# A diffusion transformer of four layers: the rotary step on three engines, modulations with their operands exchanged, and an MLP that may begin beside attention

## The chip, the cores and the metric

The kernel runs on one core of one Trainium2 chip. A core has five engines with instruction queues of their own: TensorE (PE, matrix products, with weight loads in a row of their own, PEld), VectorE (DVE), ScalarE (ACT, activation functions from tables), GpSimd (POOL) and SyncE (SP, which here only issues DMAs). Each takes its queue in order and waits on semaphores for the others. TensorE writes to PSUM, eight banks of 128 x 512 floats. The metric is the device time of one execution in microseconds, the median of three.

## The reference, cut to what matters

Sixteen samples of 256 tokens and width 256 pass through four layers in sequence. All have 16 heads of 16 columns and are computed in fp32; a context of 77 tokens per sample feeds the cross attentions.

```python
# layer 0: modulated norm, masked self attention with rotary position, cross attention, MLP
x_norm = _ln(x, norm1_w) * (1 + sc_msa) + sh_msa
q, k = _apply_rope(q, cos, sin), _apply_rope(k, cos, sin)
x = x + g_msa * self_out;  x = x + g_x * cross;  x = x + g_mlp * mlp_out
# layer 1: modulated cross attention          layer 2: self attention, cross attention, MLP, modulated
# layer 3: the rotary layer again, with rotary queries and keys in the cross attention too
q = _rope((xn @ q_w.T).reshape(B, L, N_HEADS, HEAD_DIM))
k = _rope((context @ k_w.T).reshape(B, L_ctx, N_HEADS, HEAD_DIM))
h = jax.nn.gelu(xn @ ffn_w1.T + ffn_b1, approximate=False)
x = res + (h @ ffn_w2.T + ffn_b2)
```

A modulation is a product of the 16 condition vectors with a 256 x 512 weight: a shift and a scale for every sample and column. A rotary step is `t * cos + swap(t) * sin`, where `swap` exchanges the two halves of each head's 16 columns (the sign lies in the sine table).

## The kernel before, in words

The work has six stages. Stage a is layer 0's attentions, b its MLP, c the attentions of layers 1 and 2, d layer 2's MLP, e layer 3's attentions, f its MLP. In a and e all 16 self attentions come first and the 16 cross attentions after them; priorities grow in that order.

The order of instructions is made by a planner (`Order`, line 71). Every step is a task with an engine, an estimated duration, dependencies, and holds on numbered buffers: `b` is the eight PSUM banks, `kq` five buffers for an attention's keys and queries or for MLP and modulation weights, `qk` four for rotated projections, `rope` two, `ec` two for exponentials or for an MLP's hidden rows, `xn`, `y` and `xr` one each. `solve` (line 101) lets the engines run in estimated time; a TensorE step is chosen by priority, others by when they became ready. The result is written out as one fixed program, so other durations or dependencies shuffle the whole program. The planner's durations know nothing of activation tables.

The steps that the change and the prediction speak of:

- **Norm of a sample** (`norm_tasks`, 476): statistics on VectorE (L460, L461), the reciprocal root (L466, L467) and scaling (L491) on GpSimd, a transpose of blocks on VectorE (L519), two DMAs through DRAM (L524, L528), and the modulation on ScalarE (L539).
- **Modulation** (`modulation`, 368): for each of four groups of 128 columns the weight is TensorE's stationary side and the 16 conditions stream (L382); VectorE adds the bias (L387, L389, L392). There are ten, `0a` to `3m`.
- **Rotary** (`rotate_tasks`, 663): projections into a bank (L619, or L684 for the 77 context tokens), then `turns` on VectorE: the product with the cosines (L696) and two with the sines (L699), all reading the bank; then `plus` on GpSimd (L704). `turn_back` (711) transposes the sum (L724), and ScalarE takes it to `kq` (L635, L651).
- **Attention** (`attention`, 731): scores for the row maxima (L844, L856; reductions L870, L874, L878), the maxima through DRAM into the operands (L888 to L895), scores again (L937), the exponential on ScalarE (L949, L951), value products (L960), division (L969 to L986), output product (L619), addition to `x_sb` (L1016, or L1026 to L1031).
- **MLP** (`mlp`, 1037): the norm waits for the norms of all attentions of the stage before (`bar0`). The first product (L1059), gelu on ScalarE (L1064) and second product (L1010) start at `open_h`, which waits for `barrier`, the join of all exponentials of the stage before. In turn the exponentials of the next stage wait for all gelus. Exponential, tanh gelu and exact gelu need three different function tables, and the load of a table is an instruction in ScalarE's queue.

The program prints the functions with the profile's line numbers:

Of the kernel before, what the change touches and what calls it, by code (L numbers as in the profile page):

```python
# [13 lines left out]
ALU = mybir.AluOpType  # L14
AX = mybir.AxisListType

B, N, D, H, HD, LC, FF = 16, 256, 256, 16, 16, 77, 1024
P = 128
# [42 lines left out]
class Task:  # L61
    __slots__ = ("eng", "dur", "run", "deps", "take", "prio", "rp", "left", "ready", "outs", "held", "start", "end", "no", "since", "kind", "more",
                 "lat", "first", "mb")
# [10 lines left out]
class Order:  # L74
# [4 lines left out]
    PATIENCE = 2.0  # L79
    FAVOUR = 3.0  # L80
    PER_MB = 2.7
    def __init__(self, caps):
# [17 lines left out]

    def solve(self):
        import heapq
        caps = self.caps
        loose = {k: list(range(n)) for k, n in caps.items()}
        free, waiting, events, result = {}, {}, [], []
# [34 lines left out]
        def choose(cand):  # L140

            lone = None
            for t in cand:
                if t.rp is None:
                    return [t]
                mates = [u for u in cand if u.rp == 1 - t.rp and room(t, u.take)]
                if mates:
                    return [t, min(mates, key=lambda u: (u.kind == t.kind, u.prio, u.no))]
                if lone is None:
                    lone = t  # L150
                    if t.since is None:
                        t.since = now
            if lone is not None and (now >= lone.since + self.PATIENCE - 1e-9 or not events):
                return [lone]
            return None

        while n_done < len(self.tasks):
            progress = True
            while progress:
                progress = False  # L160
                for eng in list(waiting):
                    if eng != "NO" and free.get(eng, 0.0) > now + 1e-9:
                        continue
                    cand = [t for t in waiting[eng] if t.ready <= now + 1e-9]
                    cand.sort(key=lambda t: (t.prio, t.no) if eng == "PE" else (not t.first, t.prio, t.no) if eng in ("SP", "NO") else
                              (not t.first, t.ready - self.FAVOUR * any(h.tag == "b" for h in t.held), t.prio, t.no))
# [28 lines left out]
def pixart_kernel(ctx: ExitStack, tc: tile.TileContext, x, cond_t, ctx_in, mask_c, mask_s, tables, vecs, rows,  # L195
# [172 lines left out]
    def modulation(name, src, col, shift_at, scale_at, c_t, bias, norm=None, gate=None, deps=(), prio=0, gprio=None):  # L368
        hw, hm, s = Hold("kq"), Hold("b"), {}
        m = mods[name] = const.tile([P, 4, B], F32, name=f"mod_{name}")  # L370
# [5 lines left out]
        def mults():  # L376
            ps = psum(hm)
            s["ps"] = ps[:, 0:4 * B].rearrange("p (s b) -> p s b", b=B)
            for i, at in enumerate((shift_at, scale_at)):
                for c in range(NC):  # L380
                    for k in range(NC):
                        nc.tensor.matmul(s["ps"][:, 2 * i + c, :], lhsT=s["w"][:, k, at + c * P:at + (c + 1) * P],  # L382
                                         rhs=c_t[:, k, :], start=(k == 0), stop=(k == NC - 1))

# [277 lines left out]
    def rotate_tasks(s, key, ws, xT, src_t, n, half, uses, name, prio):  # L662
# [6 lines left out]
        for group in ([list(range(nt))] if len(ws) == 1 else [[t] for t in range(nt)]):  # L669
# [16 lines left out]

            def turns(group=group, u=u, hr=hr):
                r1 = u["r1"]
                r2 = u["r2"] = buf(hr)
                hn = width // HD  # L690
                for i, t in enumerate(group):
                    tt = (t * P % half) // P
                    pv, v1, v2 = (a[0:r, i * width:(i + 1) * width].rearrange("q (h w) -> q h w", w=HD)
                                  for a in (u["p"], r1, r2))
                    cs = tabT[0:r, tt, 0, :].unsqueeze(1).to_broadcast([r, hn, HD])
# [341 lines left out]
    def mlp(b, name, wv, h_w, w_t, eps, mod, func, b1, pre_add, gate, prio, barrier, before):  # L1037
# [343 lines left out]
```

## Time and profile before

| | |
|---|---|
| median of 3 runs | 2617.77 us (2614.37 to 2619.29) |
| the profiled execution | 2619.31 us, span 2617.4 us |
| mean granted TensorE clock | 0.991 |
| GpSimd scaling L491 | 320 of 1469 ns |
| rotary add L704, 128x512 | 80 of 1276 ns |
| rotary products L696, 128x512; L699, 128x256 | 64 of 681 ns; 128 of 414 ns |
| modulation product L382 | 160 recorded passes, median 263 ns |
| copy of a bank by ScalarE, 128x512 (L1024) | 16 of 575 ns |
| table loads | 6 of 1283 ns |

An fp32 matmul shows as two recorded passes. A busy time counts a pass with its latency, so overlapping passes are merged in sums and not in means. Some matmul records are missing from a trace. An instruction's name is its line in the kernel, its output tile and its inputs. Times in the timeline are from the start of the span.

### The profile page before, as it was taken

How to read it: one execution, taken by the hardware profiler on the slowest of the kernel's cores; microseconds unless marked ns; L12 is line 12 of the kernel's file. 1: busy time of each engine (PE TensorE's matmuls, PEld its weight loads, DVE VectorE, ACT ScalarE, POOL GpSimd, SP SyncE). 2: the span in 40 equal slices, each digit the busy share in tenths (PEclk: the TensorE clock that was granted, in tenths of full speed). 3: DMA queues.
4: the chain of work that ended last, by engine and by line, in shares of the span. 5: the costliest groups of instructions: out<-in, count | busy, mean ns of one | idle time of the engine just before them, and what ended most of it. 6: DMA issues, size and time to landing. Idle time of an engine off the chain costs nothing. (4 is left out here: it accounts for less than half of the span.)

```text
span 2617.4 us, 71563 instructions
## 1 busy us (share of the span) xinstructions
PE 2562.5 (98%) x29192; PEld 1677.9 (64%) x29192; DVE 1596.0 (61%) x4489; ACT 1284.3 (49%) x2559; POOL 1138.9 (44%) x1429
## 2 busy tenths in 40 slices
PE   8999999999999899999999999999999999998999
PEld 4555555556888656555556567888555555566888
DVE  6788886775130567777777784111878887885100
ACT  2555555564333456565556564232455555554322
POOL 5344434566552355333335566432233334557310
PEclk9999999999999899999999999999999999999999
DMA  5110111224221121111111123111100001121110
GB/s 173 31 32 26 35 33 40 69 79 136 69 78 53 40 70 51 57 52 40 40 41 46 55 79 106 60 61 41 36 28 28 28 28 38 46 77 57 57 57 29
DMA packets 159809, 144.08 MB, mean 55 GB/s; under 512 B 24648, under 2 KB 124216, under 8 KB 158712
## 3 DMA queue, kind: packets, MB, share of 16 engines
q1 hardware_dynamic: 159480, 139.51, 17.1%
q8 instruction: 229, 3.75, 0.6%
q14 instruction: 100, 0.82, 0.1%
HBM read 91.86 MB, written 47.61 MB: 53 GB/s over the span
## 5 line engine op out<-in xcount | busy, mean ns | idle before, releaser
L951 ACT ACTIVATE ec<-bank 128x512 f32<-128x512 f32 (+1 forms) x1152 | 611.6, 596 | 505.1 <-PE bank L844 300.2
L937 PE MATMUL bank<-kq 32*128 32x256 f32 (+1 forms) x5120 | 638.3, 395 | 4.9 <-ACT ec L949 2.7
L491 POOL TENSOR_SCALAR xn<-x_sb,mv,rstd 128x256 f32<-128x256 f32 x320 | 452.6, 1469 | 112.4 <-DVE y L519 101.3
L937 PEld LDWEIGHTS bank<-kq 32*128 32x128 f32 (+1 forms) x5120 | 360.3, 167 | 186.5 <-issue 96.7
L844 PE MATMUL bank<-kq 32*128 32x512 f32 x1536 | 446.8, 634 | 1.6 <-ACT ec L951 0.8
L874 DVE TENSOR_REDUCE mx<-bank 128x2 f32<-128x512 f32 x544 | 342.3, 680 | 59.3 <-PE bank L844 58.2
L1064 ACT ACTIVATE ec<-bank,vec 128x256 f32<-128x256 f32 x384 | 159.9, 467 | 403.1 <-PE bank L1059 365.5
L960 PE MATMUL bank<-ec,v 128*32 128x256 f32 (+1 forms) x5120 | 351.7, 385 | 5.2 <-ACT ec L951 2.9
L1059 PE MATMUL bank<-xT,kq 128*128 128x256 f32 x1536 | 344.1, 381 | 0.0
L1010 PE MATMUL bank<-kq,ec 128*128 128x256 f32 x1536 | 340.2, 379 | 0.0
L1059 PEld LDWEIGHTS bank<-xT,kq 128*128 128x128 f32 x1536 | 291.9, 191 | 42.1 <-issue 2.8
L1010 PEld LDWEIGHTS bank<-kq,ec 128*128 128x128 f32 x1536 | 291.2, 190 | 41.3 <-issue 2.1
L982 POOL TENSOR_TENSOR od<-ts,rec 128x128 f32<-128x128 f32 x448 | 170.9, 403 | 319.5 <-DVE rec L976 319.3
L519 DVE STREAM_TRANSPOSE y<-xn 128x512 f32<-128x512 f32 x158 | 110.6, 700 | 306.9 <-DMA yd<-y 255.2
L960 PEld LDWEIGHTS bank<-ec,v 128*32 128x32 f32 (+1 forms) x5120 | 156.4, 110 | 158.6 <-issue 39.4
L878 DVE TENSOR_REDUCE mx<-bank 128x4 f32<-128x308 f32 x512 | 211.6, 468 | 41.5 <-PE bank L937 30.0
L870 DVE CUSTOM_DVE_ANT_0 junk<-bank,ctx 128x256 f32<-128x256 f32 x448 | 189.0, 422 | 51.6 <-PE bank L844 22.1
L969 DVE STREAM_TRANSPOSE ts<-bank 128x512 f32<-128x512 f32 x224 | 157.8, 705 | 68.0 <-PE bank L960 57.9
L466 POOL TENSOR_SCALAR rstd<-mv 128x2 f32<-128x2 f32 x160 | 37.9, 237 | 352.8 <-DVE mv L461 281.3
L704 POOL TENSOR_TENSOR qk<-qk,rope 128x512 f32<-128x512 f32 (+1 forms) x96 | 113.7, 1185 | 175.5 <-DVE rope L699 118.7
L856 PE MATMUL bank<-kq 32*128 32x154 f32 x2048 | 166.4, 307 | 3.3 <-ACT ec L951 1.1
L844 PEld LDWEIGHTS bank<-kq 32*128 32x128 f32 x1536 | 136.6, 183 | 40.0 <-ACT ec L951 24.6
(162 smaller groups left out, 3255.9 us busy)
## 6 DMA issues: line engine op xcount, KB each, us to landing
yd<-y SPq DMA_DIRECT2D x158, 256.0 KB
xr<-yd SPq DMA_DIRECT2D x158, 256.0 KB
kq<-in_mod_dram SPq DMA_DIRECT2D x10, 512.0 KB
cin<-in_ctx_in_dram SPq DMA_DIRECT2D x36, 128.0 KB
x_sb<-in_x_dram SPq DMA_DIRECT2D x16, 256.0 KB
gb<-gate_g0m SPq DMA_DIRECT2D x16, 256.0 KB
gb<-gate_g2a SPq DMA_DIRECT2D x16, 256.0 KB
gb<-gate_g2m SPq DMA_DIRECT2D x16, 256.0 KB
```

The costliest lines, as they stand in the source:

```text
L491: nc.gpsimd.tensor_scalar(to, of, s["mv"][:, t, 0:1], s["rstd"][:, t:t + 1], ALU.subtract, ALU.mult)
L844: ls.append(lambda ps=ps, R=R, keys=keys: nc.tensor.matmul(ps.rearrange("p (s k) -> p s k", k=N), lhsT=s["qx"][R, 0, g, t * P:(t + 1) * P] ...
L856: ls.append(lambda ps=ps, R=R, keys=keys, tt=tt: nc.tensor.matmul(ps[:, 2 * tt * n:2 * (tt + 1) * n].rearrange("p (s k) -> p s k", k=n), l ...
L870: nc.vector.tensor_tensor_reduce(junk, u[i][:, i2 * N:(i2 + 1) * N], mb[:, t, :], -1.0, 3.0e38, ALU.add, ALU.min, m[:, i2, g, t:t + 1])
L874: nc.vector.tensor_reduce(m[:, :, g, t], u[i].rearrange("p (s k) -> p s k", k=N), AX.X, ALU.max, negate=True)
L878: nc.vector.tensor_reduce(m[:, :, g].rearrange("p s t -> p t s"), u[i][:, 0:4 * n].rearrange("p (t s k) -> p t s k", s=2, k=n), AX.X, ALU. ...
L937: (lambda ps=u[i], R=R, q=q: nc.tensor.matmul(ps[0:rows_n, q * N:(q + 1) * N], lhsT=s["kz"][R, q, g, kc * P:kc * P + rows_n], rhs=s["qx"][ ...
L951: nc.scalar.activation(e, u[i][0:rows_n], AF.Exp)
L960: nc.tensor.matmul(u5["p"][32 * r:32 * r + 32, 1 - q, :], lhsT=s["v"][0:rows_n, kc, 8 * g + 2 * r + 1 - q, :], rhs=s["e", g, kc, r][0:rows ...
L982: nc.gpsimd.tensor_tensor(ov[:, :, HD * i:HD * i + HD], ts[:, i, :, HD * i:HD * i + HD], rec[:, i, :].unsqueeze(2).to_broadcast([P, N // 3 ...
L1010: nc.tensor.matmul(u["p"][:, t, :], lhsT=lhsT(k, t), rhs=w()[:, k, :], start=(k == 0), stop=(k == nk - 1))
L1059: nc.tensor.matmul(u["p"][:, j, :], lhsT=wv["w1"][:, k, f * P:(f + 1) * P], rhs=s["xT"][:, k, :], start=(k == 0), stop=(k == NC - 1))
```

## The change

Three edits, one program.

1. Rotary: the bank is copied to SBUF by ScalarE, which frees the bank; GpSimd multiplies with the sines from the copy; after it VectorE multiplies the copy by the cosines in place; GpSimd adds as before. The planner's durations follow.
2. Modulation: the 16 conditions become the stationary side and the 512 weight columns stream, into a 16 x 512 bank; ScalarE copies it, TensorE transposes four blocks back, VectorE adds the bias as before.
3. `open_h` of every MLP no longer waits for `barrier`.

`solve` also gains a seed that shakes priorities; it is called without one, and then `rank` is the priority as it was.

```diff
 def modulation(name, src, col, shift_at, scale_at, c_t, bias, ...):
-        hw, hm, s = Hold("kq"), Hold("b"), {}
+        hw, hr_, hc, hm, s = Hold("kq"), Hold("b"), Hold("tmp"), Hold("b"), {}
...
         def mults():
-            ps = psum(hm)
-            s["ps"] = ps[:, 0:4 * B].rearrange("p (s b) -> p s b", b=B)
+            for k in range(NC):
+                nc.tensor.matmul(psum(hr_)[0:B], lhsT=c_t[:, k, :], rhs=s["w"][:, k, :], start=(k == 0),
+                                 stop=(k == NC - 1))
+
+        def copy():
+            s["r"] = buf(hc).rearrange("b t d -> b (t d)")
+            nc.scalar.copy(s["r"][0:B], psum(hr_)[0:B])
+
+        def turn():
+            s["ps"] = psum(hm)[:, 0:4 * B].rearrange("p (s b) -> p s b", b=B)
             for i, at in enumerate((shift_at, scale_at)):
                 for c in range(NC):
-                    for k in range(NC):
-                        nc.tensor.matmul(s["ps"][:, 2 * i + c, :], lhsT=s["w"][:, k, at + c * P:at + (c + 1) * P],
-                                         rhs=c_t[:, k, :], start=(k == 0), stop=(k == NC - 1))
+                    nc.tensor.transpose(s["ps"][:, 2 * i + c, :], s["r"][0:B, at + c * P:at + (c + 1) * P],
+                                        ident[0:B, 0:B])
...
-        t1 = add("PE", 2.0, mults, deps=[t0], take=[hm], use=[hw], prio=prio)
+        t1 = add("PE", 0.95, mults, deps=[t0], take=[hr_], use=[hw], prio=prio)
+        t1 = add("ACT", 0.6, copy, deps=[t1], take=[hc], use=[hr_], prio=prio)
+        t1 = add("PE", 0.4, turn, deps=[t1], take=[hm], use=[hc], prio=prio)
...
 def rotate_tasks(s, key, ws, xT, src_t, n, half, uses, name, prio):
-            def turns(group=group, u=u, hr=hr):
...
-                    nc.vector.tensor_tensor(v1, pv, cs, ALU.mult)
...
-                        nc.vector.tensor_tensor(v2[:, :, 8 * z:8 * z + 8], pv[:, :, 8 - 8 * z:16 - 8 * z], sn,
-                                                ALU.mult)
+            def copy(u=u, w_all=w_all):
+                nc.scalar.copy(u["r1"][0:r, 0:w_all], u["p"][0:r, 0:w_all])
...
+            def sines(group=group, u=u, hr=hr):
+                u["r2"] = buf(hr)
+                for v1, v2, tt in views(u, group):
                     for z in range(2):
                         sn = tabT[0:r, tt, 1, 8 * z:8 * z + 8].unsqueeze(1).to_broadcast([r, hn, 8])
+                        nc.gpsimd.tensor_tensor(v2[:, :, 8 * z:8 * z + 8], v1[:, :, 8 - 8 * z:16 - 8 * z], sn, ALU.mult)
+
+            def cosines(group=group, u=u):
+                for v1, v2, tt in views(u, group):
+                    nc.vector.tensor_tensor(v1, v1, tabT[0:r, tt, 0, :].unsqueeze(1).to_broadcast([r, hn, HD]), ALU.mult)
...
-            d = add("DVE", 0.75 * size, turns, deps=[a, tab_t], take=[hr], use=[hm, hq], prio=prio)
+            a = add("ACT", 0.3 * size, copy, deps=[a], use=[hm, hq], prio=prio)
+            d = add("POOL", 0.65 * size, sines, deps=[a, tab_t], take=[hr], use=[hq], prio=prio)
+            d = add("DVE", 0.35 * size, cosines, deps=[d], use=[hq], prio=prio)
             out_t.append(add("POOL", 0.65 * size, plus, deps=[d], use=[hr, hq], prio=prio))
...
 def mlp(b, name, wv, h_w, w_t, eps, mod, func, b1, pre_add, gate, prio, barrier, before):
-        t_h = add("NO", 0.0, open_h, deps=[xT_t, w_t["w1"], barrier], take=[he], prio=prio)
+        t_h = add("NO", 0.0, open_h, deps=[xT_t, w_t["w1"]], take=[he], prio=prio)
```

More of the change, by code (lines that the diff above doesn't have):

```diff
@@ L61 @@
 class Task:
-    __slots__ = ("eng", "dur", "run", "deps", "take", "prio", "rp", "left", "ready", "outs", "held", "start", "end", "no", "since", "kind", "more",
+    __slots__ = ("eng", "dur", "run", "deps", "take", "prio", "rp", "left", "ready", "outs", "held", "start", "end", "no", "since", "kind", "more", "rank",
                  "lat", "first", "mb")
@@ L80 @@
     FAVOUR = 3.0
+    CHANCE = 4.0
     PER_MB = 2.7
@@ L99, in add, with solve @@
         return t
-    def solve(self):
+    def solve(self, seed=0):
         import heapq
+        import random
+        rng = random.Random(seed)
         caps = self.caps
+        for t in self.tasks:
+            t.rank, t.left, t.ready, t.since = t.prio + self.CHANCE * rng.random() * (seed > 0), len(t.deps), 0.0, None
+            for h in t.held:
+                h.no, h.users = -1, 0
+        for t in self.tasks:
+            for h in t.held:
+                h.users += 1
         loose = {k: list(range(n)) for k, n in caps.items()}
@@ L147, in choose @@
                 if mates:
-                    return [t, min(mates, key=lambda u: (u.kind == t.kind, u.prio, u.no))]
+                    return [t, min(mates, key=lambda u: (u.kind == t.kind, u.rank, u.no))]
                 if lone is None:
@@ L164, in solve @@
                     cand = [t for t in waiting[eng] if t.ready <= now + 1e-9]
-                    cand.sort(key=lambda t: (t.prio, t.no) if eng == "PE" else (not t.first, t.prio, t.no) if eng in ("SP", "NO") else
+                    cand.sort(key=lambda t: (t.rank, t.no) if eng == "PE" else (not t.first, t.prio, t.no) if eng in ("SP", "NO") else
                               (not t.first, t.ready - self.FAVOUR * any(h.tag == "b" for h in t.held), t.prio, t.no))
@@ L685, in mm, with views @@
                                              rhs=w()[:, k, :], start=(k == 0), stop=(k == NC - 1))
-            def turns(group=group, u=u, hr=hr):
-                r1 = u["r1"]
-                r2 = u["r2"] = buf(hr)
-                hn = width // HD
+            def copy(u=u, w_all=w_all):
+                nc.scalar.copy(u["r1"][0:r, 0:w_all], u["p"][0:r, 0:w_all])
+            def views(u, group):
                 for i, t in enumerate(group):
[L692 to L695, printed above, removed]
-                    nc.vector.tensor_tensor(v1, pv, cs, ALU.mult)
+                    v1, v2 = (a[0:r, i * width:(i + 1) * width].rearrange("q (h w) -> q h w", w=HD)
+                              for a in (u["r1"], u["r2"]))
+                    yield v1, v2, (t * P % half) // P
+            hn = width // HD
+            def sines(group=group, u=u, hr=hr):
+                u["r2"] = buf(hr)
+                for v1, v2, tt in views(u, group):
                     for z in range(2):
                         sn = tabT[0:r, tt, 1, 8 * z:8 * z + 8].unsqueeze(1).to_broadcast([r, hn, 8])
-                        nc.vector.tensor_tensor(v2[:, :, 8 * z:8 * z + 8], pv[:, :, 8 - 8 * z:16 - 8 * z], sn,
-                                                ALU.mult)
+                        nc.gpsimd.tensor_tensor(v2[:, :, 8 * z:8 * z + 8], v1[:, :, 8 - 8 * z:16 - 8 * z], sn, ALU.mult)
+            def cosines(group=group, u=u):
+                for v1, v2, tt in views(u, group):
+                    nc.vector.tensor_tensor(v1, v1, tabT[0:r, tt, 0, :].unsqueeze(1).to_broadcast([r, hn, HD]), ALU.mult)
             def plus(u=u, w_all=w_all):
```

## The prediction

> **What bounds the kernel now.** I read the page's busy shares first, then the granted clock and GpSimd's row in the 40 slices.
>
> ```profile
> PE 2562.5 (98%) x29192; PEld 1677.9 (64%) x29192; DVE 1596.0 (61%) x4489; ACT 1284.3 (49%) x2559; POOL 1138.9 (44%) x1429
> ...
> POOL 5344434566552355333335566432233334557310
> PEclk9999999999999899999999999999999999999999
> ```
>
> TensorE is busy 98% of the span, so at most 2617.4 - 2562.5 = 54.9 us of idle time can be filled; ScalarE, VectorE and GpSimd have room on average. The question is where the 54.9 us lie. I asked for busy time by stretch and took the places where TensorE falls below 95%. Columns: stretch, length, then busy time and count of TensorE, its weight loads, VectorE, ScalarE, GpSimd; granted clock; DMA.
>
> ```profile
> 580.00:632.00 52.00, 45.72 (x536) 25.77 (x536) 37.76 (x119) 27.96 (x50) 42.74 (x64) 0.87 0.30 90
> 860.00:890.00 30.00, 20.96 (x183) 15.37 (x175) 14.15 (x28) 8.75 (x18) 14.45 (x11) 0.83 0.16 53
> 1556.00:1600.00 44.00, 40.85 (x548) 24.26 (x548) 35.16 (x112) 24.07 (x50) 35.93 (x53) 1.00 0.35 119
> 1824.00:1850.00 26.00, 24.48 (x337) 14.12 (x336) 21.15 (x46) 9.19 (x19) 14.09 (x14) 1.00 0.20 64
> 2355.00:2392.00 37.00, 28.16 (x371) 17.04 (x361) 27.61 (x89) 15.03 (x29) 34.85 (x45) 0.91 0.21 70
> 0.00:30.00 30.00, 20.71 (x224) 13.31 (x228) 21.15 (x57) 5.25 (x10) 20.75 (x30) 1.00 0.88 284
> ```
>
> Three of them are the seams where attention ends and an MLP begins: idle 6.3 (a to b), 3.1 (c to d) and 8.8 us (e to f), 18.3 in all. The clock takes more: 0.13 x 52 = 6.8 and 0.09 x 37 = 3.3, together 10.1. So the seams hold 28.4 us. The other two seams (MLP to attention, at 870 and 1830) and the start hold 9.0, 1.5 and 9.3 us idle, and the last slice after the final matmul 3.9. Between these places the attention stages leave TensorE about 13 us idle in some 2000, so nothing that only relieves VectorE there can be worth much. The waits and GpSimd's timeline of the last seam show its mechanism:
>
> ```profile
> PE bank L724 <- POOL qk L704: 5.4, 1, 5.4
> ```
> ```profile
> 2364.59 2.79 POOL L491 TENSOR_SCALAR xn<-x_sb,mv,rstd 128x256 f32<-128x256 f32 x2
> 2367.26 1.26 POOL L704 TENSOR_TENSOR qk<-qk,rope 128x512 f32<-128x512 f32 x1
> ```
>
> The last rotated query stands in GpSimd's queue behind two MLP norms, and TensorE has nothing to put in its place: the MLP, whose inputs are being prepared, waits for the last exponential.
>
> **The change: MLP without the barrier.** The first matmuls of the MLP no longer wait for the last exponential. In the built order the first gelu of each seam now stands 16 exponentials (two attentions) before the last. I walked the last seam through that order with durations of this trace, from the end of the last attention input's modulation (time 0). TensorE: projections to 2.5, earlier attention 10.4 more (values 2.1, output 1.9, scores 4.3, values 2.1), now five MLP groups of 4 matmuls, 8 x 0.216 = 1.73 each (8.6), output 1.9: it reaches the last query's transposes at 23.4. GpSimd to the same point: 2.1 until the first norm, four norms of 2.8, five reciprocal roots of 0.95, two bias adds of 1.28, sines 1.7, two divisions of 0.76, the add 1.27; 25.1 in sum. So TensorE idles some 1.7 where it idled 5.4; with stalls before the last value products I leave 4 of 8.8. In the first seam the eight matmuls that want a whole MLP hidden row wait about 2 for its fourth gelu pair; I leave 4 of 6.3. In the middle seam I leave 3 of 3.1. Idle gain 18.3 - 11 = 7.3. The clock fell only in the two seams with gaps of several us; with none above 2 I let 1.1 of its 10.1 remain: gain 9.0. Sum **-16.3**. At worst nothing is gained, at best 28.4.
>
> The removed barrier also kept two activation functions apart. The built order has 18 table loads where there were 6: 12 more. Queued behind each on ScalarE are exponentials for which value products wait, or gelus for which the second MLP matmul waits. The row:
>
> ```profile
> 1855.21 0.65 ACT L811 COPY v<-bank 128x256 f32<-128x256 f32 x2 [3.08 <-PE bank L619]
> 1855.87 1.28 ACT L951 ACT_TABLE_LOAD   x1
> 1858.05 1.08 ACT L951 ACTIVATE ec<-bank 128x512 f32<-128x512 f32 x2 [0.90 <-PE bank L844]
> ```
>
> A load takes 1.28 and starts as the copy ends; the 0.9 after it is put down to TensorE. 12 x 1.28 = 15.4 us of ScalarE. The Trainium skill (ScalarE: Activation LUTs, "What ACT_TABLE_LOAD costs") speaks against the change: it adds a drain of some 1.38 to each switch, 2.66 in all, so 12 x 2.66 = 31.9. The row shows no such drain before the load, so I take 1.28. The walk has room for that: in the last seam the first value products come 3.6 after their scores (output 1.9, MLP group 1.7), and load, four exponentials and a hop need 1.28 + 2.05 + 0.3 = 3.6. With the page's price each such place would be 1.4 short, 12 x 1.38 = 16.6, and the forecast below would become 2625.
>
> **Rotary.** Removed from VectorE (L696, L699): 64 tiles of 0.68 + 2 x 0.41, 16 query groups of two 0.41 + four 0.28, 16 key groups of 0.40 + two 0.28: 97 + 31 + 15 = 143 by means, 134 of merged busy time. Added: ScalarE copies, 64 x 0.575 (row L1024), 16 x 0.575, 16 x 0.37, 52 us; VectorE cosines from SBUF, nearest row the 128x1232 product of two SBUF tensors (L1224, 1.42): 1.15 ns an element, some 0.62 a tile and 0.35 for 256, about 57; GpSimd sines, none in the trace: between L982 (128 strided elements 0.40) and L704 (77x256 0.73), so 0.70 for 256 and 0.42 for 128: 64 x 1.4 + 16 x (1.7 + 0.84) = 130. Totals become ScalarE 1284 + 52 + 5 + 15 = 1356, VectorE about 1519, GpSimd 1269 (48%): none bounds. What changes is a chain, TensorE to add: before 1.5 + 1.3, now 0.6 + 1.4 + 0.6 + 1.3, 1.1 us and one or two queue hops longer. Inside a stage other attentions cover that. At the start nothing does: the order puts four sines of 1.4 into GpSimd's queue, and the add that releases the first transposes moves from 28.4 to about 33; but 32 projection matmuls (3.7) that followed the first scores now precede them. Net +1.5 (bounds 0 and 6). Stage e starts likewise behind a running MLP: +1.
>
> Here too the skill has a rule against the change (GPSIMD Engine Reference, "Key points"): GpSimd contends with VectorE instructions that have two SBUF inputs. The trace agrees where L1224 and L1225 run:
>
> ```profile
> 876.01 1.33 POOL L466 TENSOR_SCALAR rstd<-mv 128x2 f32<-128x2 f32 x1 [1.21 <-DVE mv L461]
> 877.42 1.88 POOL L467 TENSOR_TENSOR rstd<-rstd,nhalf 128x2 f32<-128x2 f32 x1
> ```
>
> Their medians elsewhere are 0.23 and 0.72, so 2.3 us lost under some 3 us of such work. The old products read PSUM; the cosines read SBUF twice. 57 us of cosines, half of them over GpSimd work, cost GpSimd 20 to 30 us. At 50% use that is covered except where GpSimd is behind, at the seam and the start: +1 by the row (without the rule 0).
>
> **Modulations (10).** Before: 16 passes of 16 columns behind 16 weight loads of 128 columns; in a dense stretch L382 starts at 663.86 and the next line at 665.56: 1.70. After: four passes of 512 columns. Nearest row L411 (same sides, 256 columns): three passes in 0.82, of which one alone is 0.38, so 0.22 a pass, 0.43 at 512, 1.72 for four; plus four transposes at the spacing of L1124 (0.65 - 0.27)/3 = 0.13, 0.5. So +0.5 each; seven lie in saturated stretches: **+3.5** (bounds -3 if passes overlap, +6). ScalarE's copy between them is in order behind gelus or exponentials, and TensorE's other groups cover it. At 870 the second one feeds the scaled context, on the path: the copy fits before VectorE's transpose that held it (to 874.1); I put +0.4. No DMA is added.
>
> Sum against the profiled execution, 2617.4 + 1.9 around the span = 2619.3: -16.3 + 1.5 + 1.0 + 1.0 + 3.5 + 0.4 = -8.9, so 2610.4. That execution lies 1.5 above the median 2617.77, so **2609**, 0.3% faster. Since every duration changes, the planner shuffles the whole order; a measurement tells 0.2% (5.2 us) from no change, and the shuffle may be worth as much either way.
>
> **The rivals.** (1) As above, own range 2602 to 2613: chance 0.35. (2) The seams fill completely and freed banks and VectorE also take half of the 13 us inside the stages: 2609 - 11 = 2598, chance 0.13. For it: VectorE is busy 196 of the first 250 us. Against: TensorE is already at 248.6 of the next 250. (3) The change moves the seams' idle time and does not remove it, since GpSimd (34.85 of 37 us busy in the last seam) sets when they end and gets more to do: 2617, chance 0.17. (4) **Slower by the table loads**: the value products in the seams wait out each load. Place: the value products after an exponential whose predecessor was a gelu. At 1.28 all twelve give 2609 + 15 = 2624; at 2.66 they give 2641. It decides once they put 14 us on TensorE: eleven bare loads, or six at the page's price. Chance 0.2. (5) GpSimd becomes the releaser inside stages a and e: in the cross-attention half of e it goes from about 55% to above 70%, in instructions of 1.4 us in order. If each of 48 rotated attentions stalls TensorE by 0.5, +24: 2633. Chance 0.15.
>
> Faster: 0.35 + 0.13 = 0.48; within 0.2%: 0.17; slower: 0.2 + 0.15 = 0.35. The range that leaves out two in ten runs from 2595 to 2632.
>
> **What would show it.** Right: TensorE idle in the three seams down from 18 to about 11 us and the clock near 1.0 there; 18 table loads with under 0.5 us of TensorE waiting on the exponentials behind each; GpSimd near 1270 to 1300 busy; a modulation's matmuls and transposes 2.2 us. Wrong: value products waiting a microsecond or more at each switch; transposes of rotated tiles waiting for GpSimd's add many times, not once; or stages a, c and e themselves changed in length by more than 5 us, which would make the shuffled order the cause.

## The result, and the profile after

The changed kernel takes 2606.28 us (median of eight runs, 2604.26 to 2611.79) where the kernel before, on the same chip, took 2618.28 (eight runs, 2614.37 to 2624.33): ratio 0.9956, 95% interval 0.9943 to 0.9968, so 0.44% faster. The forecast was 2609. Its profiled execution took 2611.8 us, the slowest of the eight, with a span of 2610.0; against the span before (2617.4) that is 7.4 us less.

The busy shares and the granted clock on the page of the changed kernel:

```profile
span 2610.0 us, 71673 instructions
...
PE 2550.0 (98%) x29112; PEld 1660.2 (64%) x29112; DVE 1550.4 (59%) x4265; ACT 1351.2 (52%) x2677; POOL 1276.9 (49%) x1653
...
PEclk9999999999999899999999999999999999999999
```

TensorE's idle time did not shrink. It grew, from 54.9 to 2610.0 - 2550.0 = 60.0 us. What became less is its busy time, by 12.5, and over half of that is clock in this pair of executions. The records of the granted clock show it at half speed in a few stretches of 3.4, 6.8 or 10.2 us. Half of each stretch is put down here as time lost: added up, 23.9 us before and 15.4 after. That is too much where TensorE had no work in the stretch anyway: of the 10.2 us at half speed in the hole at 870 it was busy for 3.7 before. Counted over its busy time alone ("the busy count" below), the loss is 18.7 before and 11.8 after, so 6.9 is a better figure than 8.5. The tables and runs below use the whole count.

Nor is the clock the same in every execution of one program. Seventeen executions of the kernel before on one chip had mean clocks from 0.994 to 0.988, a loss of 16 to 31 us each, and took 2610.0 to 2626.3 us. By the mean clocks of all recorded executions the changed kernel lost 16.6 us (eight executions) and the kernel before 18.4, 19.2 and 22.3 (46 executions on three chips). On average, then, the clock is 2 to 6 of the 12 us. The clock figures of a single trace, here and in the experiments, tell where it fell in that execution, and not what an edit is worth to it.

The busy time by stretch of the changed kernel, at the three seams and, second, at the seam from stage b to c. Columns as in the prediction: stretch, length, busy time and count of TensorE, weight loads, VectorE, ScalarE, GpSimd; granted clock; DMA.

```profile
590.00:650.00 60.00, 53.48 (x537) 33.72 (x532) 41.48 (x127) 35.94 (x63) 51.90 (x78) 0.94 0.31 94
860.00:900.00 40.00, 30.91 (x296) 22.56 (x299) 23.82 (x55) 15.32 (x32) 14.63 (x11) 0.87 0.13 43
1556.00:1610.00 54.00, 50.24 (x555) 31.60 (x544) 34.60 (x108) 32.48 (x59) 41.65 (x60) 1.00 0.28 91
2340.00:2400.00 60.00, 56.18 (x583) 38.43 (x579) 37.61 (x113) 34.15 (x63) 53.20 (x70) 0.97 0.32 103
```

These stretches are some us longer than the prediction's and not cut at the same work. In them the three seams hold 6.5, 3.8 and 3.8 us idle, 14.1 where the prediction's held 18.3, and lose 0.06 x 60 + 0.03 x 60 = 5.4 to the clock where those lost 10.1. The hole at 870 is as it was: 40.00 - 30.91 = 9.1. TensorE's longest waits in the changed kernel (line that waits, what ended the wait; total, times, longest):

```profile
PE bank L648 <- DVE ctx L1253: 7.2, 2, 5.0
PE bank L639 <- DVE oT L1014: 6.4, 3, 4.8
...
PE bank L752 <- POOL qk L730: 4.8, 4, 2.0
...
PE bank L752 <- ACT ec L979: 3.4, 1, 3.4
```

The 5.4 us wait for the last rotated query is gone. New is a wait of 4.8 for VectorE's transpose of an attention's output (L1014) at 608, in the first seam; the hole at 870 now ends with the scaled context (L1253) and no longer with a norm, as it did before:

```profile
PE bank L619 <- ACT xT L539: 8.3, 2, 7.8
```

Both programs cut at the same counts of value products and MLP products give this account (us; "clock" is the time lost at half speed):

| stretch | idle before, after | clock before, after |
|---|---|---|
| start, to a tenth of stage a | 9.3, 10.1 | 0, 3.4 |
| inside a | 1.5, 2.5 | 3.4, 0 |
| seam a to b, to the middle of b | 7.4, 9.3 | 6.8, 3.4 |
| seam b to c (the hole at 870) | 10.5, 10.4 | 10.2, 5.1 |
| inside c | 3.8, 5.7 | 0, 0 |
| seam c to d | 3.1, 3.8 | 0, 0 |
| d, and the start of e | 2.2, 1.1 | 0, 0 |
| inside e | 4.2, 9.2 | 0, 1.7 |
| seam e to f | 9.1, 4.0 | 3.4, 1.7 |
| end of f | 3.9, 3.9 | 0, 0 |
| sum | 54.9, 60.0 | 23.9, 15.4 |

The remaining busy time, with the clock's loss taken off, fell from 2538.6 to 2534.7: 3.9. So +5.1 - 8.5 - 3.9 makes the 7.4 (rounded). By the busy count it is +5.1 - 6.9 - 5.7. No run shows what made the remaining busy time shorter. The seams' figures depend on the cut: a hole some us earlier or later goes to another row. The account also covers the traced executions alone: the other 4 to 5 us of the 12 are in no trace.

### The profile page after: what moved, and what is told of

The parts are those of the page before. It is cut to its first block, busy times and chain, and to the rows that moved or that the text cites. A ratio compares the mean times of both kernels' runs of the same rounds, so it can differ in the third digit from the quotient of the medians.

```text
span 2610.0 us, 71673 instructions
## 1 busy us (share of the span) xinstructions
PE 2550.0 (98%) x29112; PEld 1660.2 (64%) x29112; DVE 1550.4 (59%) x4265; ACT 1351.2 (52%) x2677; POOL 1276.9 (49%) x1653
## 4 chain that ended last, share of the span: by engine, by line
PE 91%; DVE 3%; POOL 2%; ACT 2%; DMA 1%; issue 1%; SPq 0%; ACTq 0%; DVEq 0%; POOLq 0%
PE bank L639 22%; PE bank L965 13%; PE bank L1087 13%; PE bank L1038 12%; PE bank L988 11%; PE bank L872 8%; PE bank L831 2%; PE bank L884 2%; PE bank L648 2%; PE bank L958 2%; PE bank L752 2%; ACT ec L979 1%; POOL xn L511 1%; DVE mx L906 1%; DMA xr<-yd 1%
## 5 line engine op out<-in xcount | busy, mean ns | idle before, releaser
L965 PE MATMUL bank<-kq 32*128 32x256 f32 (+1 forms) x5120 | 631.6, 394 | 1.1 <-DVE mx L902 0.6
L511 POOL TENSOR_SCALAR xn<-x_sb,mv,rstd 128x256 f32<-128x256 f32 x320 | 457.9, 1485 | 106.2 <-DVE y L539 97.5
L872 PE MATMUL bank<-kq 32*128 32x512 f32 x1536 | 436.0, 633 | 1.2 <-ACT ec L979 1.0
L988 PE MATMUL bank<-ec,v 128*32 128x256 f32 (+1 forms) x5120 | 346.0, 383 | 3.0 <-ACT ec L977 1.4
L1010 POOL TENSOR_TENSOR od<-ts,rec 128x128 f32<-128x128 f32 x448 | 172.5, 406 | 241.6 <-DVE rec L1004 241.2
L722 POOL TENSOR_TENSOR rope<-qk,tabT 128x256 f32<-128x256 f32 (+2 forms) x224 | 135.0, 627 | 139.3 <-ACT qk L708 129.0
L1059 POOL TENSOR_TENSOR x_sb<-x_sb,tmp 128x512 f32<-128x512 f32 x80 | 101.8, 1273 | 134.3 <-DVE tmp L1054 132.9
```

What stands on the lines that cost most here:

```text
L511: nc.gpsimd.tensor_scalar(to, of, s["mv"][:, t, 0:1], s["rstd"][:, t:t + 1], ALU.subtract, ALU.mult)
L872: ls.append(lambda ps=ps, R=R, keys=keys: nc.tensor.matmul(ps.rearrange("p (s k) -> p s k", k=N), lhsT=s["qx"][R, 0, g, t * P:(t + 1) * P] ...
L965: (lambda ps=u[i], R=R, q=q: nc.tensor.matmul(ps[0:rows_n, q * N:(q + 1) * N], lhsT=s["kz"][R, q, g, kc * P:kc * P + rows_n], rhs=s["qx"][ ...
L988: nc.tensor.matmul(u5["p"][32 * r:32 * r + 32, 1 - q, :], lhsT=s["v"][0:rows_n, kc, 8 * g + 2 * r + 1 - q, :], rhs=s["e", g, kc, r][0:rows ...
```

## The experiments

Each run is compared with runs of the kernel before on the same chip; those medians were 2612.61, 2620.19 and 2615.58 us in the three groups of four, so ratios are what to compare. "In us" below is a ratio's distance from 1 times 2618.

### Each edit alone, and two together

The rotary edit alone, the modulation edit alone, the barrier alone, and the changed kernel with the barrier put back. The diffs are the parts of the change; the third is

```diff
-        t_h = add("NO", 0.0, open_h, deps=[xT_t, w_t["w1"], barrier], take=[he], prio=prio)
+        t_h = add("NO", 0.0, open_h, deps=[xT_t, w_t["w1"]], take=[he], prio=prio)
```

Rotary alone:

> The kernel before with the rotary edit alone (copy on ScalarE, sines on GpSimd, cosines on VectorE), the barrier and the old modulations kept. Theory 1, the prediction's own terms: start +1.5, stage e +1, contention +1, so 3.5 us slower than before, about 2621.8 against 2618.3. Theory 2, reordering: with the new durations the planner writes 1025 switches of TensorE between tile shapes (tiles of 32 rows, tiles of 32 columns, whole array) where before has 1057; if a switch costs what the planner estimates, 0.13 to 0.2 us, it is 4 to 6 us faster, about 2613. Theory 3, GpSimd becomes the releaser in stages a and e: 15 or more slower, above 2633.

Measured: 2627.61 against 2612.61, ratio 1.006 (1.0045 to 1.0076), 15.7 us slower. Only theory 3's size fits ("15 or more slower"), and its mechanism is not there: GpSimd is busy 1277.1 us, and TensorE's waits for a rotated tile come to 6.0 us in four waits, not to one for every rotated attention. In its trace the last seam went from 9.1 idle and 3.4 clock to 16.3 and 10.2 (+14.0), the start by 2.3 and 5.1 (+7.4), the inside of stage e by 3.6 and 1.7 (+5.3); busy time at full clock fell by 9.3. A gain of theory 2's size is there (its cause was not tested), and is more than paid back at the last seam.

Modulation alone:

> The kernel before with the modulation edit alone. Theory 1, the prediction's terms: +3.5 for seven modulations in saturated stretches and +0.4 at the start of stage c: 3.9 slower, about 2622. Theory 2, reordering: 16 more switches of tile shape (1073 for 1057) of 0.13 to 0.2, 2 to 3 slower through them alone; together with theory 1 about 2624. A rival: the five-step chain (matmul, copy, transposes, add) delays nothing and the passes overlap, up to 3 faster, 2615.

Measured: 2612.13, ratio 0.9993 (0.9984 to 1.0001): no measurable difference, the rival's side of zero. The 3.9 us of theory 1 are not there.

No barrier alone:

> The kernel before with one edit: the MLP's first hidden row no longer waits for the last exponential. Theory 1: 16.3 faster through the seams (idle -7.3, granted clock -9.0), about 2602, and the loads of function tables hidden. Theory 2: the loads are paid, six extra or more at 1.28, and the seam's idle time is only moved: between 0 and 8 faster, 2610 to 2618. Reordering adds 33 switches of tile shape, 4 to 6 us against the edit, if they cost what the planner puts.

Measured: 2603.39, ratio 0.996 (0.9947 to 0.9972), 10.5 faster, between the two theories. The trace shows another cause than either. The last seam did not gain: idle 9.1 to 10.7, clock 3.4 to 5.1. The first gained 2.6 idle and 5.1 clock. The hole at 870, at which nothing was changed, went from 10.5 idle and 10.2 clock to 2.3 and 3.4: 15 us, or 12 by the busy count. One task has moved its place, and a run further down tests whether that is the reason. Modulation 1k scales the context of layer 1's cross attention; in the kernel before VectorE writes it at 874.12 (line 387), in this one at 686.77. The line of the kernel before, and then the timeline of the kernel without the barrier:

```profile
874.12 0.18 DVE L387 TENSOR_TENSOR mod_1k<-bank,vec 128x64 f32<-128x64 f32 x1
```

```profile
674.91 0.57 SPq L385 DMA_DIRECT2D kq<-in_mod_dram  x1
683.96 1.85 PE L393 MATMUL bank<-scondT,kq 128*128 128x16 f32 x16
686.77 0.21 DVE L398 TENSOR_TENSOR mod_1k<-bank,vec 128x64 f32<-128x64 f32 x1
```

The barrier's removal shuffled the planner's order so that 1k's weight was loaded at 675 in place of 866. Why the buffer went to it then was not traced back.

Rotary and modulation with the barrier:

> The changed kernel with the barrier put back: rotary and modulation edits without the third. Theory 1: 3.5 + 3.9 = 7.4 slower than before, about 2625.7; and the changed kernel itself then owes its whole 12 us to the missing barrier, which would be worth 19 on top of these two. Theory 2, reordering: 1021 switches of tile shape against 1057, 5 to 7 faster, about 2612; the missing barrier is then worth only 6 on top of these two.

Measured: 2621.9, ratio 1.003 (1.0018 to 1.0043), 7.9 slower: theory 1's 7.4, but as 15.7 - 1.8 and an interaction of -6, not as 3.5 + 3.9. Theory 2 falls. On top of these two, the missing barrier is worth 7.9 + 11.5 = 19.4 us, twice what it is worth alone.

### What the missing barrier does beside the rotary edit

The timeline of the kernel with rotary and modulation edits and the barrier, at the last seam:

```profile
2356.70 0.64 PE L639 MATMUL bank<-w_e,oT 128*32 128x256 f32 x8 [0.23 <-DVE oT L1014]
...
2361.01 2.79 POOL L511 TENSOR_SCALAR xn<-x_sb,mv,rstd 128x256 f32<-128x256 f32 x2
2363.68 0.76 POOL L1010 TENSOR_TENSOR od<-ts,rec 128x128 f32<-128x128 f32 x2
2364.40 1.27 POOL L730 TENSOR_TENSOR qk<-qk,rope 128x512 f32<-128x512 f32 x1
...
2364.99 2.79 PE L639 MATMUL bank<-w_e,oT 128*32 128x256 f32 x24 [7.65 <-DVE oT L1014]
```

The division of an attention (L1010) stands on GpSimd behind the MLP's norms (L511), the rotated query's add (L730) behind the division, and TensorE waits 7.65 us with nothing to put in. In the changed kernel the same place reads:

```profile
2365.50 8.90 PE L1087 MATMUL bank<-xT,kq 128*128 128x256 f32 x40
...
2369.93 2.81 POOL L511 TENSOR_SCALAR xn<-x_sb,mv,rstd 128x256 f32<-128x256 f32 x2
...
2372.61 0.77 POOL L1010 TENSOR_TENSOR od<-ts,rec 128x128 f32<-128x128 f32 x2
...
2374.33 1.93 PE L639 MATMUL bank<-w_e,oT 128*32 128x256 f32 x32
```

GpSimd still has the division behind the norms, but 40 passes of the MLP's first product, 8.9 us, fill TensorE until it is done. To see how much of the 19.4 lies here, the barrier was taken away in stage f's MLP alone, once on top of the two edits and once on the kernel before:

```diff
-        ... deps=[xT_t, w_t["w1"], barrier] ...
+        ... deps=[xT_t, w_t["w1"], barrier if name != "f" else None] ...
```

> Rotary and modulation edits with the barrier taken away in stage f's MLP only. With the barrier everywhere these two gave ratio 1.003, without it 0.9956, 19 us apart. Theory D: the two edits lengthen the chain of the last rotated attentions, the barrier at the last seam exposes it, and most of the 19 lie there (idle 15.6 to 4.0, clock 6.8 to 1.7 in the two traces): 15 to 17 faster than with the barrier, ratio 0.9965 to 0.9975. Prediction's theory: the three seams gain in proportion to what they hold, so this seam alone 8 or less, ratio 1.0 or above.

Measured: 2607.48, ratio 0.9969 (0.9957 to 0.998), 8.1 faster than before. From 1.003 that is 16 us, of the 19.4 that all three barriers are worth: theory D's number. That most of the gain lies at this seam is shown; that the longer chain is what the barrier exposes there is read from the two timelines. The last seam reads 3.6 idle and no lost clock.

> The kernel before with the barrier taken away in stage f's MLP only. The prediction's walk: the seam's 8.8 idle become 4 and its clock loss of 3.3 nearly goes, 7 to 8 faster, ratio 0.997. Theory D: without the rotary edit this seam waits for the last query (5.4 us behind GpSimd's add) whether or not the MLP may begin, as the trace with all barriers gone shows it (idle 10.7, clock 5.1): between 4 faster and 5 slower, ratio 0.9985 to 1.002.

Measured: 2621.39, ratio 1.0025 (1.0013 to 1.0037), 6.5 us *slower*. The prediction's walk falls for this order, and theory D's range ended short of it. Its timeline:

```profile
2363.75 1.26 POOL L715 TENSOR_TENSOR qk<-qk,rope 128x512 f32<-128x512 f32 x1
2365.07 1.11 PE L735 MATMUL bank<-ident,qk 128*128 128x128 f32 x4 [5.38 <-POOL qk L715]
...
2370.36 1.99 PE L1070 MATMUL bank<-xT,kq 128*128 128x256 f32 x8
...
2376.97 1.28 ACT L1075 ACT_TABLE_LOAD   x1
...
2379.12 1.28 ACT L962 ACT_TABLE_LOAD   x1
2381.06 1.55 PE L971 MATMUL bank<-ec,v 77*32 77x256 f32 x16 [1.89 <-ACT ec L962]
```

The first MLP product (L1070) stands behind the transposes of the last query (L735) in TensorE's queue, so the 5.38 us wait is what it was. After it gelus and exponentials alternate one by one: nine loads from 2372 on, where the kernel before has one, and here value products do wait (1.89 at this place, 4.2 in four waits over the seam). Idle went from 9.1 to 10.7 and clock from 3.4 to 5.1 there. Idle and clock at this seam make 3.3 of the 6.5 us; where the rest lies was not traced. So removing the barrier at this seam did not help in the old order, and helped by 16 us in the order that the rotary and modulation edits bring about.

### The other two pairs

> The changed kernel with the old modulation: rotary edit and missing barrier. The three edits taken alone gave +15.0, -0.5 and -9.2. Theory A, the edits add up: 5.8 slower than before, ratio 1.002. Theory B, the place of one modulation decides: in the kernel without the barrier alone, modulation 1k came at 687 us, inside stage b, and the hole of 8 us at 870 closed; in this program it lies at the same place (before the modulation of layer 1's queries is followed by four MLPs), and no barrier waits at the seam to stage f: 8 idle and some 5 of clock less than the changed kernel at 870, so 13 faster than the changed kernel, ratio 0.9905 to 0.992 to before. Theory C, the modulation edit pays for itself whatever the order: slower than the changed kernel, ratio 0.996 to 0.998.

Measured: 2596.48 against 2620.19, ratio 0.9916 (0.99 to 0.9932), 22 us faster. Theory B's number, and **this version beats both kernels**: 0.4% below the changed one. Its trace is of the slowest of its six executions (2605.6). Its stretches at the first seam, the hole at 870 and the last seam:

```profile
590.00:650.00 60.00, 57.67 (x552) 39.60 (x551) 33.63 (x99) 30.86 (x55) 40.79 (x54) 1.00 0.32 100
...
860.00:900.00 40.00, 38.01 (x410) 25.92 (x402) 22.75 (x64) 17.22 (x37) 12.87 (x15) 0.96 0.22 65
2340.00:2400.00 60.00, 56.27 (x538) 39.11 (x530) 37.20 (x112) 32.12 (x59) 54.84 (x70) 0.97 0.25 81
```

Idle 2.3, 2.0 and 3.7 us: here all the holes are small at once. On top of this version the modulation edit costs 10.5 us (between two ratios that are each known to about 0.0015, or 4 us), and the trace of the changed kernel shows two holes that it brings back, 6.5 against 2.3 at the first seam and 9.1 against 2.0 at 870.

> The changed kernel with the old rotary step: modulation edit and missing barrier. Theory A, the edits add up: -0.5 - 9.2 = 9.7 faster than before, ratio 0.9963. Theory B: in this program modulation 1k stands after the last MLP of stage b again, so the hole at 870 stays open (10 idle, 5 clock) and the missing barrier gains only at the two other seams: 0 to 4 faster than before, ratio 0.9985 to 1.0.

Measured: 2610.86, ratio 0.9965 (0.9952 to 0.9978), 9.2 faster. The sum of theory A fits (0.9963); theory B's number does not, though what it says of the trace holds: 1k is written at 871.6 and the hole at 870 keeps 9.7 idle. The gain lies elsewhere (the clock at 870 loses 5.1 in place of 10.2, the last seam's idle is 6.3 in place of 9.1), so a sum that fits is not a cause found.

With these two, every combination of the three edits has been run. The missing barrier is worth 10.5 us on the kernel before, 7 with the modulation edit, 38 with the rotary edit and 19.4 with both: a gain each time, and of very different size. Neither of the other edits gains on the kernel before.

### Whether one modulation's place is the cause

```diff
-    modulation("1k", mod1, 512, 256, 0, scondT, "m1k", **when(3))
+    modulation("1k", mod1, 512, 256, 0, scondT, "m1k", **when(1))
```

> The kernel before with none of the three edits: only modulation 1k is made due with modulation 1q, in the middle of stage b, in place of after the last MLP of that stage. Theory B, the hole at 870 us is the wait for it and for the scaling of the context that follows: idle -8 there and 5 to 7 of half clock, 13 to 15 faster, ratio 0.9945 to 0.995; that is as much as the whole change brings. Rival: the last MLP's own norm and the next attention's norm hold TensorE there, and the hole stays: ratio 1.0.

Measured: 2607.15, ratio 0.9965 (0.9953 to 0.9978): 9.2 us from this one line, four fifths of what the whole change brings, and short of the 13 expected. At 870 the seam lost 5.6 idle and all 10.2 of the clock (7.0 by the busy count); 3.4 of clock came back at the first seam and as much at the third. Busy time by stretch, first in this kernel and then in the changed one:

```profile
850.00:890.00 40.00, 38.72 (x401) 29.09 (x404) 17.99 (x50) 19.03 (x40) 13.40 (x14) 1.00 0.19 56
```
```profile
850.00:890.00 40.00, 30.98 (x247) 22.70 (x246) 15.79 (x31) 12.84 (x27) 15.89 (x12) 0.87 0.15 47
```

The timeline of the changed kernel shows what TensorE waits for in that hole:

```profile
865.19 0.59 SPq L385 DMA_DIRECT2D kq<-in_mod_dram  x1
...
869.33 1.89 PE L389 MATMUL bank<-kq,scondT 128*16 128x512 f32 x4 [0.58 <-DMA kq<-in_mod_dram]
...
871.94 0.42 PE L400 MATMUL bank<-ident,tmp 16*128 16x16 f32 x4 [0.72 <-ACT tmp L394]
873.59 0.19 DVE L405 TENSOR_TENSOR mod_1k<-bank,vec 128x64 f32<-128x64 f32 x1
...
877.32 0.71 PE L648 MATMUL bank<-ctx,w_c 128*128 128x77 f32 x2 [4.96 <-DVE ctx L1253]
```

From weight load to scaled context the chain takes 12 us, and it starts only as the last products of stage b run.

> The changed kernel, all three edits, with modulation 1k made due with 1q. Theory B: the hole at 870 closes as in the kernel above, 8 idle and up to 5 clock less; in this order the seam to stage d waits some 5 longer instead, so 3 to 8 faster than the changed kernel, ratio 0.9925 to 0.9945. If the modulation edit's cost in the kernel with all three edits (ratio 0.9956 against 0.9916 without it) is not the place of 1k but its matmuls and its chain, the ratio stays at 0.9956.

Measured: 2606.07, ratio 0.9963 (0.995 to 0.9977), no different from the changed kernel's 0.9956. The hole closed as foreseen (10.4 idle and 5.1 clock became 2.0 and 0), yet the time did not move: the seam to stage d took 1.8 idle and 3.4 clock more, and TensorE's busy time at full clock rose by 8.1 (2534.7 to 2542.8; by the busy count 5.8). **What in the order costs those 6 to 8 us stays open.** So 1k's place is shown to be worth 9 us in the kernel before, and not shown to be what the modulation edit costs in the kernel with all three.

### The table loads

The changed kernel and the kernel before are run with gelu replaced by the identity, which needs no table of its own; the MLP then computes without its gelu. An activation of 128 x 256 takes 467 ns (median) with the identity and 466 with gelu, so on ScalarE only the loads differ. The drain of 1.38 in the first expectation is the page's figure that the prediction names.

```diff
-    ... AF.Gelu_apprx_tanh, "b1_0" ...   ... AF.Gelu, "b1_3" ...
+    ... AF.Identity, "b1_0" ...          ... AF.Identity, "b1_3" ...
```

> The changed kernel with the MLP's gelu replaced by the identity function in all three MLPs, which needs no table of its own (so the MLP computes without its gelu). 17 of the 18 table loads go. Theory 1, the loads are hidden: within 3 us of the changed kernel, ratio to before 0.9945 to 0.9968. Rival, the bare loads are waited out by the value products: 12 x 1.28 = 15 faster than the changed kernel, ratio 0.990; with a drain of 1.38 beside each load 32 faster, ratio 0.984.

Measured: one table load in place of 18, ratio 0.9951 (0.9938 to 0.9965), against 0.9956 with them: no difference, to some 5 us. The 15 us of the bare loads and the 32 with a drain are excluded; theory 1 holds.

> The kernel before with the identity function in place of gelu in all three MLPs (the MLP computes without its gelu): five of its six table loads go. It says what the identity itself and five loads at seams with a barrier are worth. Theory 1: loads at a barrier lie in the open, 5 x 1.28 = 6.4 faster at most, ratio 0.9975; if the identity's shorter activations matter, more. Rival: no difference, since two of the five loads were issued while ScalarE waited.

Measured: 1.0001 (0.9989 to 1.0012); the rival holds, and the five loads at barriers cost nothing that shows either (the interval ends at 3 us).

## Why the prediction was right, and where not

The sum was -8.9 on the profiled execution and -7.4 was measured there; on medians 12.0 where 9 was forecast. The number is better than its terms, which missed on both sides and cancelled. By the account above:

| term of the prediction | predicted | measured in the span |
|---|---|---|
| three seams without the barrier | -16.3 | -7.6 |
| 12 table loads | 0 | 0 |
| start | +1.5 | +4.2 |
| inside stage e | +1.0 | +6.7 |
| contention on GpSimd | +1.0 | not separable |
| hole at 870 (b to c) | +0.4 | -5.2 |
| busy time at full clock (modulations) | +3.5 | -3.9 |
| insides of a, c and d | 0 | -1.6 |
| sum | -8.9 | -7.4 |

By the busy count the seams read -6.2, the hole -4.8 and the busy time at full clock -5.7; the other rows stay.

**The barrier.** At the last seam the walk was right that the 5.4 us wait for the last rotated query would go. That 4.0 were left where it left 4 is luck: they are almost all one other wait, 3.4 us before the transposes of an earlier query, at a time when no MLP product could stand in for them. Every traced kernel with the rotary edit has this wait (2.5 to 4.0 us), and none without it:

```profile
2350.28 0.76 PE L752 MATMUL bank<-ident,qk 128*128 128x128 f32 x6 [3.43 <-ACT ec L979]
```

The step that failed is the same figure for the first seam: it left 4 of 6.3 by way of the wait for a hidden row, but what holds TensorE there is an attention's output in the old queue, 4.8 us, before any MLP input exists; 6.5 remained:

```profile
608.77 2.79 PE L639 MATMUL bank<-w_a,oT 128*32 128x256 f32 x24 [4.76 <-DVE oT L1014]
609.46 1.09 ACT L559 ACTIVATE xT<-xr,mod_0m 128x256 f32<-128x256 f32 x2 [7.55 <-DMA xr<-yd]
```

The clock, from 10.1 to 1.1 by the prediction, came to 5.4. The prediction read the trace as if the clock fell only at gaps of several us. In the trace before, 13.6 of the 23.9 us lie in stretches that had no hole of TensorE over 1.1 us in the 12 us ahead of them; this is one, with TensorE busy throughout and a mean clock of 0.66:

```profile
908.00:923.00 15.00, 15.00 (x152) 9.57 (x152) 9.72 (x29) 4.77 (x10) 6.55 (x9) 0.66 0.13 42
```

The version without the modulation edit, whose seams hold 2.3, 2.0 and 3.7 us idle, still lost 18.8 us in its traced execution. So closing the gaps did not bring the clock back, and what sets it there stays open. The premise of the barrier's term, that the barrier's worth can be read from the seams before, fell with the kernel in which only the last seam's barrier is gone: 6.5 us slower there, 16 faster with the other two edits.

**The table loads** cost nothing measurable in the changed kernel, as the walk said, and the run with the identity shows it. The Trainium skill (ScalarE: Activation LUTs, "What ACT_TABLE_LOAD costs") puts 1.38 of drain beside the 1.28 of a load. ScalarE's timeline in the changed kernel shows none on either side of it:

```profile
614.97 0.84 ACT L1092 ACTIVATE ec<-bank,vec 128x256 f32<-128x256 f32 x2 [3.12 <-PE bank L1087]
615.83 1.28 ACT L977 ACT_TABLE_LOAD   x1
617.12 2.41 ACT L977 ACTIVATE ec<-bank,kbT 77x512 f32<-77x512 f32 x4
```

The load starts 0.02 us after the gelu's end and the next exponential 0.01 after the load. The rival was real all the same: in the order of the kernel before with only the last seam's barrier gone, value products waited 1.89 us for an exponential that stood behind such a load. Whether loads hide is a property of the order.

**The rotary edit** was sized 3.5 in all (start, stage e, contention). Alone it measured 15.7. The chain was worked out rightly, but "other attentions cover that" stops at the last seam, where there are none: it cost 14.0 there. In the changed kernel the third edit covers the 7.65 us wait for the division, though not the 3.4 us one. In what remained, the start (+4.2, 3.4 of it clock) and the inside of stage e (+6.7) were still three and seven times too small. The engine totals came out as predicted for ScalarE (1351 for 1356) and GpSimd (1277 for 1269 to 1300), but not for VectorE (1550 for 1519), of which the last section tells.

**The modulations.** The size was right. In a dense stretch of the changed kernel:

```profile
667.61 1.89 PE L389 MATMUL bank<-kq,scondT 128*16 128x512 f32 x4 [0.98 <-DMA kq<-in_mod_dram]
669.43 1.99 PE L1087 MATMUL bank<-xT,kq 128*128 128x256 f32 x8
...
674.80 0.42 PE L400 MATMUL bank<-ident,tmp 16*128 16x16 f32 x4
675.15 3.72 PE L1038 MATMUL bank<-kq,ec 128*128 128x256 f32 x16
```

From start to next start 1.82 and 0.35, 2.17 us in sum where 2.2 was predicted and 1.70 was before. But seven times +0.5 is not what the edit did to the time: alone it measured -1.8 us, within the noise, and on top of the other two +10.5. The order that it led to must have counted for more; which part of the order did is not shown.

**The shuffle.** The prediction gave it "as much either way" as 5.2 us and left it out of the sum. It was the largest unpriced term. Over the programs here, which do the same products but for the modulations, TensorE's busy time at full clock lay between 2528.6 and 2542.8 us (2533.7 and 2546.3 by the busy count), and the hole at 870 between 2 and 10.5 idle. The prediction had named a sign for the shuffled order as the cause, stages a, c and e changed by more than 5 us; in stage e 6.7 us more are lost. So the direction was forecast for reasons that hold only in part: the last seam (shown), the hidden loads (shown), and the clock, whose 8.5 for 9.0 is luck: half of it lies in other places, and on the average of all executions it is 2 to 6.

## What to carry to other kernels

Where a planner writes the order of the program, judge an edit by the program it leads to, and test edits in combination: here +15.7, -1.8 and -10.5 us alone made -11.5 together, and the best of the tested programs left one of the three out. A wait that seems to hold a seam is worth what other work the order can put in its place, so look in the queue of the new program for what stands ahead of the waiting instruction. And ask of every hole why its chain starts so late: one line that made a modulation due earlier brought 9 us to the kernel before, and nothing measurable to the changed one.

## What the hardware showed that was not expected

The prediction let the contention of VectorE's cosines with GpSimd fall on GpSimd, 20 to 30 us of its time. It fell on both, and mostly on VectorE: all its cosines took 78 us busy where 57 were predicted. Groups of the changed kernel (count | busy us, mean ns | idle before, releasers):

```profile
L511 POOL TENSOR_SCALAR xn<-x_sb,mv,rstd 128x256 f32<-128x256 f32 x320 | 457.9, 1485 | 106.2 <-DVE y L539 97.5 <-DVE rec L1004 0.9
...
L730 POOL TENSOR_TENSOR qk<-qk,rope 128x512 f32<-128x512 f32 x80 | 102.5, 1282 | 34.7 <-DVE qk L726 27.0 <-PE bank L639 3.8 <-PE bank L872 3.2
...
L726 DVE TENSOR_TENSOR qk<-qk,tabT 128x512 f32<-128x512 f32 x64 | 49.6, 778 | 15.8 <-POOL rope L722 15.8
```

The norm (L511) had a mean of 1469 ns before, the add 1276: hardly more now. A cosine product was put at 620 ns and takes 778. It depends on what GpSimd runs when it starts, as the timeline of the start shows:

```profile
24.39 3.41 POOL L511 TENSOR_SCALAR xn<-x_sb,mv,rstd 128x256 f32<-128x256 f32 x2
24.44 0.69 DVE L726 TENSOR_TENSOR qk<-qk,tabT 128x512 f32<-128x512 f32 x1 [2.30 <-POOL rope L722]
...
29.02 1.27 POOL L730 TENSOR_TENSOR qk<-qk,rope 128x512 f32<-128x512 f32 x1
29.10 1.74 DVE L726 TENSOR_TENSOR qk<-qk,tabT 128x512 f32<-128x512 f32 x1 [0.56 <-POOL rope L722]
```

Started 0.08 us into GpSimd's add of two SBUF tensors, it took 1.74 us in place of 0.69, and the add lost nothing: VectorE's product all but waited until the add was over. Started into a norm, which reads one tensor, it lost nothing, and it was the norm that took longer (3.41 for two, elsewhere 2.81; 35 norms with a cosine product beside them have a mean of 1627 ns, the others 1467).

Over the 64 products of this size, by what ran on GpSimd as they started: 676 ns with nothing (32), 655 with a norm (15), 1261 with an add (11), 6 with others. The mean of the eleven hides two kinds. Six began in the add's first 0.08 us, took 1.73 to 1.76 and ended 0.55 us after it; five began in its last 0.13 and took 0.65 to 0.69. Of the fifteen, twelve began in the norm's last 0.36 us; two began at its start, and the norm took 2.0 us in place of 1.47; one began 0.5 us into it, and neither lost anything.

The Trainium skill (SBUF — State Buffer, "SBUF: two separate sides") has the pair of ports that the two engines share as a lock, held for a whole instruction by whichever starts first. The add's case agrees; in the norm's case the second to start was not blocked in any of the fifteen, so the measurement decides there, on few cases with a long overlap.
